# Group-norm means moved by one attention group, the start of the kernel reordered, and part of the last image's final convolution brought forward

## The chip, the cores and the metric

One core of one Trainium2 chip runs the kernel. The metric is device time in microseconds (us), lower is better.

The engines are named as in the profile: PE multiplies matrices, PEld loads its weights, DVE is VectorE, ACT is ScalarE, POOL is GpSimd, SP issues most DMAs.

## The reference

Eight images of 512 channels and 32 x 32 pixels pass through a group norm, a convolution block with two attention bottlenecks, and a residual addition. Everything is float32.

```python
def _L0_conv_ref(x, cv1_w, cv1_bn, cv2_w, cv2_bn, m_cv1_w, m_cv1_bn, m_qkv_w, m_rw, m_rh, m_cv2_w, m_cv2_bn):
    B, C1, C2, N, F, HEADS, E = (8, 512, 512, 2, 32, 4, 0.5)
    # C = 256, HD = 64; cbs = silu(batch norm(convolution))
    t = cbs(x, cv1_w, cv1_bn, 0)                       # 1x1, 512 -> 512
    ys = [t[:, :C], t[:, C:]]
    for i in range(N):
        yi = ys[-1]
        z = cbs(yi, m_cv1_w[i], m_cv1_bn[i], 1)        # 3x3, 256 -> 256
        z = bot_attention(z, m_qkv_w[i], m_rw[i], m_rh[i])   # 4 heads, 1024 positions
        z = silu(bn_eval(conv2d(z, m_cv2_w[i], 0), m_cv2_bn[i]))
        ys.append(yi + z)
    return cbs(concatenate(ys, axis=1), cv2_w, cv2_bn, 0)    # 1x1, 1024 -> 512

x = x + _L0_conv_ref(_gn(x), ...)      # _gn: 32 groups of 16 channels
```

## The kernel before

The kernel is a chain of stages, image by image: cv1 (1 x 1), a 3 x 3 convolution, attention, m2 (1 x 1), again a 3 x 3 convolution, attention and m2, then cv2. The 3 x 3 convolution is done in a transformed domain: `make_u` transforms the weights into "filters" (`u_new`), `tiles_in` transforms the image into "tiles" (`v_in`), PE multiplies the two, and `columns_out` and `rows_out` transform back. In image 0 the filters are made on DVE and ACT and stored; later images load them. An attention has four groups (pairs of heads by halves of the positions) of some 15 us each; between groups the function `ahead` slips in work for the next image, above all its group norm. `tc.issue_after(ins)` puts a block of instructions behind `ins` in the order in which the scheduler issues. A wait is always inferred from the data and is not written.

The group norm is a generator; each `yield` is a point where one attention group has passed:

```python
        def gn_mean(mv):
            ps = ps_big.tile([P, NX], F32, tag="big", name="gm_ps")
            nc.tensor.matmul(ps, gmat, mv[:, :, 0], start=True, stop=True)
            ...
        def group_norm(xts):
            ...
            stats(range(NX // 2))
            yield
            stats(range(NX // 2, NX))
            gm, dev = gn_mean(mv)          # PE needs the statistics just queued on DVE
            yield
            gr = gn_rstd(dev)
            apply(range(NX // 2), gm, gr)
            yield
            yield apply(range(NX // 2, NX), gm, gr)
```

The start. POOL issues sixteen small loads of BatchNorm parameters before it makes `gmat`, the matrix of the group means; the BatchNorm factors are computed before the group norm is emitted:

```python
    for i, src in enumerate(bn_chunks):          # 16 chunks
        nc.gpsimd.dma_start(bnp[:, i, :], src)
    ...
    ident = const.tile([P, P], F32, name="ident")
    make_identity(nc, ident)
    ...
    gmat = const.tile([P, P // GROUP, GROUP], F32, name="gmat")
    nc.gpsimd.memset(gmat, 1.0 / GROUP)
    ...
    nc.vector.tensor_scalar(rstd, bnp[:, :, 3], BN_EPS, None, ALU.add)
    nc.gpsimd.tensor_tensor(rstd, rstd, mhalf[:, :NBN], ALU.pow)
    nc.vector.tensor_tensor(sh, bnp[:, :, 0], rstd, ALU.mult)
    ...
    with tc.issue_after([*s.group_norm(xs)][-1].ins):
        make_all(0, 0)                           # filters of the first output half
    y0 = new_y0()
    s.cv1(w1, xs, y0, ypad[0], [*Y1S, *Y0S])
    vs = s.tiles_in(ypad[0])                     # free to mix with the filters
```

The last operation of `tiles_in` (output columns 0 and 3 of the transform in one instruction) and the products for V:

```python
                    tt(v[..., 0::3], pairs_of(0), pairs_of(2), ALU.subtract)
    ...
                for j in range(per):
                    for k in range(NM):
                        nc.tensor.matmul(
                            ps[:, j, :], z[:, k, ts(j0 + j, P)], qkv_sb[:, n, k, 2 * C : 3 * C],
                            start=(k == 0), stop=(k == NM - 1),
                        )
```

In an image that is not the last, pieces of the next image's cv1 (`first`, `second`, and two more behind m2) fill the end of the first attention. The last image has nothing to put there:

```python
        def first():
            nonlocal nxt
            if more:
                nxt = new_y0()
                s.cv1(w1, xs, nxt, y1n, Y1S[: NM // 2])
        def second():
            if more:
                s.cv1(w1, xs, nxt, y1n, Y1S[NM // 2 :])
        ...
        ao, check = s.attention_fast(0, z, ..., {**{g: ahead for g in range(NG)}, NG: first, NG + 1: second})
        last = s.m2(0, ao, y1, lambda oc, half: inner(y2, oc, half))
        if more:
            s.cv1(w1, xs, nxt, y1n, Y0S)
        vs = s.tiles_in(y2)
        ...
        z = s.conv3x3(1, vs, u_of(1))
```

## Time and profile before

| | before |
|---|---|
| time, median of 3 runs | 2547.76 us (2543.94 to 2548.48) |
| span of the profiled run, granted clock | 2543.0 us, 0.989 |
| PE busy, PE idle | 2436.7 us, 106.3 us |
| cv1 of image 0 begins | 25.04 us |
| first projections (end of the first 3 x 3 convolution) begin | 89.60 us |

PE is busy 96% of the span, so the question is where its 106 us of idleness lie and what each costs. The prediction shows those views. The group of the outer-column operation, by its form (count, busy time in us, mean ns of one), shows 1065 ns where the two inner columns, of half its size, take 421:

```profile
L330 DVE TENSOR_TENSOR v_in<-w_rows 128x512 f32<-128x512 f32 x96 | 102.3, 1065 | 0.0
```

The busy times of one stretch, from the first filter operation to the end of the first tiles (from:to, its length, then busy us and instructions of PE, PEld, DVE, ACT and POOL, the granted clock, the DMA share and GB/s), show DVE 30.16 of 33.31 us busy, 3.2 us idle, and the statistics row shows when the third of the four x tiles had come:

```profile
27.07:60.38 33.31, 33.31 (x106) 17.11 (x105) 30.16 (x69) 13.88 (x27) 2.40 (x11) 1.00 0.55 194
...
8.72 1.29 DVE L373 BATCH_NORM_STATS2 st<-x 128x6 f32<-128x512 f32 x2 [1.46 <-DMA x<-in_x_dram]
```

### The profile page before, as it was taken

The page shows a single profiled execution, that of the slowest core. Times are in us where ns is not written, and L with a number is a line of the kernel's source. Part 1 is how long each engine was busy: PE and PEld are TensorE (multiplying, and loading weights), DVE is VectorE, ACT ScalarE, POOL GpSimd, SP SyncE. Part 2 cuts the span into 40 slices and gives each one's busy share as a digit, 9 for nine tenths or more (in the row PEclk, how much of TensorE's full clock was granted, in tenths as well). Part 3 has the DMA queues.
Part 4 walks back from the last instruction along what each step waited for, and adds up shares of the span by engine and source line. Part 5 has one row for each costly group of instructions (what it writes and reads, how often), then busy time and mean ns, then how long its engine had stood idle before and what let it go on. Part 6 is the DMA issues. An engine that isn't in the chain of part 4 may idle for free.

```text
span 2543.0 us, 35923 instructions
## 1 busy us (share of the span) xinstructions
PE 2436.7 (96%) x14626; PEld 1213.0 (48%) x14626; DVE 1521.0 (60%) x2524; ACT 966.6 (38%) x1322; POOL 115.0 (5%) x379
## 2 busy tenths in 40 slices
PE   6889999999999999999999999999999999999898
PEld 3535446363463634536354363634536354363533
DVE  6678564765556664656556665566564665636662
ACT  2353522525234261343514434153432535326251
POOL 2000000000100001000010000100001000000001
PEclk9999999999999999999999999999999999999999
DMA  6223114040140402304032030502205021050101
GB/s 213 76 88 136 44 37 167 15 150 10 54 150 15 149 15 75 125 15 149 15 128 76 24 136 15 189 15 77 86 10 199 10 86 40 26 182 15 50 15 60
DMA packets 86188, 199.37 MB, mean 78 GB/s; under 512 B 32384, under 2 KB 42112, under 8 KB 73728
## 3 DMA queue, kind: packets, MB, share of 16 engines
q1 hardware_dynamic: 73696, 151.35, 17.4%
q0 software_dynamic: 12320, 45.66, 5.1%
q8 instruction: 117, 1.92, 0.3%
q14 instruction: 55, 0.45, 0.1%
HBM read 166.89 MB, written 30.08 MB: 77 GB/s over the span
## 4 chain that ended last, share of the span: by engine, by line
PE 81%; DVE 8%; ACT 4%; issue 2%; DMA 1%; SPq 0%; ACTq 0%; POOL 0%; DVEq 0%
PE ps L272 31%; PE av_ps L509 14%; PE l_ps L483 13%; PE c_ps L677 12%; PE m_ps L698 4%; PE v_ps L449 4%; ACT pt L487 3%; PE s_ps L526 2%; DVE acc L495 1%; DVE ao L517 1%; DVE st L373 1%; DMA rs<-r_dram 1%; ACT t L260 1%; ACT z L260 1%; DVE r_ends L364 0%
## 5 line engine op out<-in xcount | busy, mean ns | idle before, releaser
L487 ACT ACTIVATE pt<-l_ps 128x1024 f32<-128x1024 f32 x512 | 496.0, 1025 | 221.6 <-PE l_ps L483 221.6
L495 DVE TENSOR_TENSOR acc<-acc,pt 128x1024 f32<-128x1024 f32 x384 | 469.8, 1223 | 141.8 <-ACT pt L487 117.1
L509 PE MATMUL av_ps<-pt,vT 64*64 64x512 f32 x4096 | 491.4, 595 | 12.6 <-DVE ao L517 11.2
L483 PE MATMUL l_ps<-q,kr 64*64 64x512 f32 x4096 | 493.7, 597 | 4.3 <-ACT pt L487 4.3
L677 PE MATMUL c_ps<-v_in,u 128*128 128x128 f32 x2688 | 305.4, 276 | 10.3 <-issue 6.6
L677 PEld LDWEIGHTS c_ps<-v_in,u 128*128 128x128 f32 x2688 | 304.5, 193 | 18.0 <-issue 13.6
L509 PEld LDWEIGHTS av_ps<-pt,vT 64*64 64x64 f32 x4096 | 154.8, 134 | 312.1 <-issue 226.0
L483 PEld LDWEIGHTS l_ps<-q,kr 64*64 64x64 f32 x4096 | 155.1, 134 | 287.3 <-issue 266.4
L272 PE MATMUL ps<-z,qkv_sb 128*128 128x512 f32 x512 | 229.3, 595 | 7.3 <-ACT z L260 7.3
L272 PE MATMUL ps<-x,w 128*128 128x512 f32 x512 | 227.9, 602 | 2.2 <-DVE x L406 2.2
L272 PE MATMUL ps<-ypad,w 128*128 128x512 f32 x512 | 227.1, 594 | 0.0
L260 ACT ACTIVATE t<-ps,bh,sh 128x512 f32<-128x512 f32 x64 | 47.1, 775 | 310.6 <-PE ps L272 190.8
L493 DVE TENSOR_TENSOR acc<-pt 128x1024 f32<-128x1024 f32 x64 | 78.4, 1226 | 137.1 <-ACT pt L487 137.1
L272 PEld LDWEIGHTS ps<-x,w 128*128 128x128 f32 x512 | 97.1, 192 | 130.9 <-issue 125.2
L440 DVE TENSOR_TENSOR kr<-ps,rw_sb 128x512 f32<-128x512 f32 x64 | 41.2, 686 | 192.9 <-PE ps L272 192.9
L272 PEld LDWEIGHTS ps<-ypad,w 128*128 128x128 f32 x512 | 96.6, 190 | 125.1 <-issue 125.1
L743 DVE TENSOR_TENSOR t<-t,x_res 128x512 f32<-128x512 f32 x64 | 43.9, 692 | 181.9 <-ACT t L260 155.9
L272 PEld LDWEIGHTS ps<-z,qkv_sb 128*128 128x128 f32 x512 | 94.7, 190 | 114.1 <-issue 91.8
L533 ACT COPY s_row<-s_ps 128x512 f32<-128x512 f32 x128 | 68.7, 589 | 149.0 <-PE s_ps L526 149.0
L272 PE MATMUL ps<-y,w 128*128 128x512 f32 x256 | 118.0, 599 | 4.3 <-ACT t L260 4.3
L337 ACT COPY m<-c_ps 128x256 f32<-128x256 f32 x96 | 35.4, 369 | 223.2 <-PE c_ps L677 223.2
L272 PE MATMUL ps<-ylast,w 128*128 128x512 f32 x256 | 117.2, 595 | 0.0
(119 smaller groups left out, 2136.8 us busy)
## 6 DMA issues: line engine op xcount, KB each, us to landing
u<-u SPq DMA_DIRECT2D x84, 1024.0 KB
w<-in_cv_w_dram SPq DMA_DIRECT2D x24, 1024.0 KB
x<-in_x_dram SPq DMA_DIRECT2D x32, 512.0 KB
x_res<-in_x_dram POOLq DMA_DIRECT2D x64, 256.0 KB, 3.8
out_dram<-t POOLq DMA_DIRECT2D x62, 256.0 KB, 2.6
u<-u_new POOLq DMA_DIRECT2D x12, 1024.0 KB, 5.1
rs<-r_dram SPq DMA_DIRECT2D x96, 128.0 KB
raw<-in_m_cv_w_dram SPq DMA_DIRECT2D x8, 576.0 KB
```

Source lines behind the costliest of these rows:

```text
L260: return nc.scalar.activation(dst, src, AF.Silu, scale=sh[:, k : k + 1], bias=bh[:, k : k + 1])
L272: nc.tensor.matmul(ps[:, half, :], w_of(k), rhs_of(k, half), start=(k == 0), stop=(k == nk - 1))
L449: nc.tensor.matmul(ps[:, j, :], z[:, k, ts(j0 + j, P)], qkv_sb[:, n, k, 2 * C : 3 * C], start=(k == 0), stop=(k == NM - 1),)
L483: nc.tensor.matmul(ps[kh * HD : (kh + 1) * HD, hd, :], kr[r, c, o : o + HD], q[r, c, ts(half, HALF)], start=True, stop=True,)
L487: exp = nc.scalar.activation(pt[:, i], ps, AF.Exp, scale=SCALE)
L493: return nc.vector.tensor_tensor(accs[g], pt[:, 0], pt[:, 1], ALU.add)
L495: ins = nc.vector.tensor_tensor(accs[g], accs[g], pt[:, i], ALU.add)
L509: nc.tensor.matmul(avs[g][hd * HD : (hd + 1) * HD, kh, :], vT[r, j, o : o + HD], pt[r, i, hd, :], start=(j == 0), stop=(j == NJ - 1),)
L526: nc.tensor.matmul(ps[hd * HD : (hd + 1) * HD, kh, :], ones[r], acc[r, hd, :], start=True, stop=True,)
L533: nc.scalar.copy(row, ps[:, kh, :])
L677: nc.tensor.matmul(ps[:, row, col, :], us[i][:, k, row, col, :], vs[i][:, k, row, col, :], start=(k == 0), stop=(k == NM - 1),)
L698: nc.tensor.matmul(pss[oc][:, half, :], m2_sb[:, n, k, ts(oc, P)], ao[:, k, ts(half, HALF)], start=(k == 0), stop=(k == NM - 1),)
```

## The change

The intent is to take PE's idle stretches out. There are five parts: (1) the group mean is taken one group after its statistics, and all four tiles are normalised in the last group; (2) at the start `gmat` comes first on POOL, the BatchNorm loads become six and move to ACT, the factors are computed behind the group norm, the first raw filter is loaded ahead of cv1's weights, and the tiles are put behind the filters; (3) the outer-column operation goes column by column; (4) the V products alternate between two banks, so that two of them need only the first half of z; (5) in the last image, the first half of three of cv2's four output blocks (`cv2_part`) is computed in and behind the first attention, kept in SBUF and added at the end. The core of the diff, with cuts:

```diff
+    raws = [load_raw(0, 0, 0, "k")]
     w1 = load_w1()
...
-    for i, src in enumerate(bn_chunks):
-        nc.gpsimd.dma_start(bnp[:, i, :], src)
+        nc.scalar.dma_start(bnp[:, at:bn_at, :], src.rearrange("(c p) f -> p c f", p=P))
...
-                    tt(v[..., 0::3], pairs_of(0), pairs_of(2), ALU.subtract)
+                    outer = v_all[:, k, :, 0::3].rearrange("p r c (t j) -> p c r t j", j=NW)
+                    tt(outer, *(pairs_of(a).rearrange("p r t j b -> p b r t j") for a in (0, 2)), ALU.subtract)
...
             stats(range(NX // 2, NX))
+            yield
             gm, dev = gn_mean(mv)
             yield
-            gr = gn_rstd(dev)
-            apply(range(NX // 2), gm, gr)
-            yield
-            yield apply(range(NX // 2, NX), gm, gr)
+            yield apply(range(NX), gm, gn_rstd(dev))
...
-                for j in range(per):
+                in_bank = per // NH
+                for j in range(in_bank):
                     for k in range(NM):
+                        for at in range(j, per, in_bank):
...
-    with tc.issue_after([*s.group_norm(xs)][-1].ins):
-        make_all(0, 0)
+    normed = [*s.group_norm(xs)][-1]
+    with tc.issue_after(normed.ins):
+        nc.vector.tensor_scalar(rstd, bnp[:, :, 3], BN_EPS, None, ALU.add)
+        nc.gpsimd.tensor_tensor(rstd, rstd, mhalf[:, :NBN], ALU.pow)
+        nc.vector.tensor_tensor(sh, bnp[:, :, 0], rstd, ALU.mult)
+        ...
+        made = make_all(0, 0)
     y0 = new_y0()
     s.cv1(w1, xs, y0, ypad[0], [*Y1S, *Y0S])
-    vs = s.tiles_in(ypad[0])
+    with tc.issue_after(made.ins):
+        vs = s.tiles_in(ypad[0])
...
         def first():
...
+            else:
+                parts[1] = s.cv2_part(w1, (y0, y1), 1)
         def second():
...
+            else:
+                parts[2] = s.cv2_part(w1, (y0, y1), 2)
...
+        else:
+            for oc in range(3, NO):
+                parts[oc] = s.cv2_part(w1, (y0, y1), oc)
```

More of the change, by code (lines that the diff above doesn't have):

```diff
@@ L112, in load_w1, with load_w2 @@
         return w
-    def load_w2():
+    def load_w2(n=2):
         nk = (2 + N) * NM // 2
-        ws = [ring([P, nk, C2], f"w2_{i}") for i in range(2)]
+        ws = [ring([P, nk, C2], f"w2_{i}") for i in range(n)]
         for i, w in enumerate(ws):
@@ L119, in load_w2, with load_raw @@
         return ws
+    def load_raw(n, oc, k, tag, bufs=1):
+        raw = act.tile([P, 9, P], F32, tag=tag, name="raw", bufs=bufs)
+        nc.sync.dma_start(raw, m_cv1_w[n, ts(k, P), :, ts(oc, P)])
+        return raw
+    raws = [load_raw(0, 0, 0, "k")]
     w1 = load_w1()
-    bn_chunks = []
+    NBN = 2 * NM + 2 * N * NM + NO
+    bnp = const.tile([P, NBN, 4], F32, name="bnp")
+    bn_at = 0
     def bn_slot(src, n):
-        at = len(bn_chunks)
-        for c in range(n):
-            bn_chunks.append(src[ts(c, P), :])
+        nonlocal bn_at
+        at = bn_at
+        bn_at += n
+        nc.scalar.dma_start(bnp[:, at:bn_at, :], src.rearrange("(c p) f -> p c f", p=P))
         return at
-    bn_cv1 = bn_slot(cv1_bn, NX)
+    bn_cv1 = bn_slot(cv1_bn, 2 * NM)
     bn_m1 = [bn_slot(m_cv1_bn[n], NM) for n in range(N)]
@@ L134 @@
     bn_cv2 = bn_slot(cv2_bn, NO)
-    NBN = len(bn_chunks)
-    bnp = const.tile([P, NBN, 4], F32, name="bnp")
-    for i, src in enumerate(bn_chunks):
-        nc.gpsimd.dma_start(bnp[:, i, :], src)
     qkv_sb = const.tile([P, N, NM, 3 * C], F32, name="qkv_sb")
@@ L149, in load_bottleneck @@
         nc.sync.dma_start(m2_sb[:, n], m_cv2_w[n].rearrange("(k p) o -> p k o", p=P))
-    ident = const.tile([P, P], F32, name="ident")
-    make_identity(nc, ident)
-    ones = const.tile([P, HD], F32, name="ones")
-    nc.gpsimd.memset(ones, 1.0)
     gmat = const.tile([P, P // GROUP, GROUP], F32, name="gmat")
@@ L169 @@
     nc.gpsimd.memset(mhalf, -0.5)
+    ones = const.tile([P, HD], F32, name="ones")
+    nc.gpsimd.memset(ones, 1.0)
     ypad = []
@@ L175 @@
         yp = const.tile([P, NM, F + 2, F], F32, name=f"ypad{n}")
-        for c in range(NM):
-            nc.gpsimd.memset(yp[:, c, 0, :], 0.0)
-            nc.gpsimd.memset(yp[:, c, F + 1, :], 0.0)
+        nc.gpsimd.memset(yp[:, :, 0, :], 0.0)
+        nc.gpsimd.memset(yp[:, :, F + 1, :], 0.0)
         ypad.append(yp)
@@ L187 @@
     rstd = const.tile([P, NBN], F32, name="rstd")
-    nc.vector.tensor_scalar(rstd, bnp[:, :, 3], BN_EPS, None, ALU.add)
-    nc.gpsimd.tensor_tensor(rstd, rstd, mhalf[:, :NBN], ALU.pow)
-    nc.vector.tensor_tensor(sh, bnp[:, :, 0], rstd, ALU.mult)
-    nc.vector.tensor_tensor(bh, bnp[:, :, 2], sh, ALU.mult)
-    nc.vector.tensor_tensor(bh, bnp[:, :, 1], bh, ALU.subtract)
-    for at in bn_m1:
-        nc.vector.tensor_scalar(sh[:, at : at + NM], sh[:, at : at + NM], 1 / 48, None, ALU.mult)
     u_dram = [
@@ L204, in new_u, with make_u @@
         return ring([P, NM, 2, NC, P], name)
-    def make_u(n, oc, k, us, tag, raw_tag, bufs=(1, 1)):
-        raw = act.tile([P, 9, P], F32, tag=raw_tag, name="raw", bufs=bufs[1])
-        nc.sync.dma_start(raw, m_cv1_w[n, ts(k, P), :, ts(oc, P)])
+    def make_u(n, oc, k, us, tag, raw, bufs=1):
         g0, g1, g2 = (raw[:, 3 * r : 3 * r + 3, :] for r in range(3))
-        tmp = act.tile([P, 5, 3, P], F32, tag=tag, name="u_tmp", bufs=bufs[0])
+        tmp = act.tile([P, 5, 3, P], F32, tag=tag, name="u_tmp", bufs=bufs)
         both, other, rows = tmp[:, 0], tmp[:, 1], tmp[:, 2:4]
@@ L231, in make_u @@
             tt(u[:, :, 1, :], ends, c1, ALU.add)
-            tt(u[:, :, 2, :], ends, c1, ALU.subtract)
+            last = tt(u[:, :, 2, :], ends, c1, ALU.subtract)
             nc.scalar.mul(u[:, :, 0, :], c0, 2.0)
@@ L236, in make_u @@
                 nc.gpsimd.dma_start(u_dram[n][oc][i], us[i])
+        return last
     def load_u(n, oc, i):
@@ L264, in table_of, with conv1x1 @@
             nc.scalar.activation(spare, zero, func)
-        def conv1x1(w_of, rhs_of, nk, ks=None, ps=None):
+        def conv1x1(w_of, rhs_of, nk, ks=None, ps=None, ends=None):
             if ps is None:
                 ps = ps_big.tile([P, NH, HALF], F32, tag="big", name="ps")
+            begin, end = ends or (0, nk - 1)
             for k in range(nk) if ks is None else ks:
@@ L272, in conv1x1 @@
                     nc.tensor.matmul(
-                        ps[:, half, :], w_of(k), rhs_of(k, half), start=(k == 0), stop=(k == nk - 1)
+                        ps[:, half, :], w_of(k), rhs_of(k, half), start=(k == begin), stop=(k == end)
                     )
@@ L446, in project @@
                 ps = ps_big.tile([P, per, C], F32, tag="big", name="v_ps")
-                for j in range(per):
+                in_bank = per // NH
+                for j in range(in_bank):
                     for k in range(NM):
-                        nc.tensor.matmul(
-                            ps[:, j, :], z[:, k, ts(j0 + j, P)], qkv_sb[:, n, k, 2 * C : 3 * C],
-                            start=(k == 0), stop=(k == NM - 1),
-                        )
+                        for at in range(j, per, in_bank):
+                            nc.tensor.matmul(
+                                ps[:, at, :], z[:, k, ts(j0 + at, P)], qkv_sb[:, n, k, 2 * C : 3 * C],
+                                start=(k == 0), stop=(k == NM - 1),
+                            )
                 for g in range(0, per, per // NH):
@@ L707, in m2, with cv2_products @@
             return last
-        def cv2_products(w2, ys, oc, ks, ps=None):
+        def cv2_products(w2, ys, oc, ks, ps=None, ends=None):
             def cat(k, half):
@@ L716, in cv2_products, with cv2_part, cv2 @@
             nk = (2 + N) * NM
-            return conv1x1(lambda k: w2[2 * k // nk][:, k % (nk // 2), ts(oc, P)], cat, nk, ks, ps)
-        def cv2(b, w2, ys, begun=None):
+            return conv1x1(lambda k: w2[2 * k // nk][:, k % (nk // 2), ts(oc, P)], cat, nk, ks, ps, ends)
+        def cv2_part(w2, ys, oc):
+            ks = range(2 * NM)
+            ps = cv2_products(w2, ys, oc, ks, ends=(ks[0], ks[-1]))
+            part = act.tile([P, HW], F32, tag="x", name="part", bufs=NX)
+            for half in range(NH):
+                nc.scalar.copy(part[:, ts(half, HALF)], ps[:, half, :])
+            return part
+        def cv2(b, w2, ys, begun=None, parts={}):
             def rows_of(dram, oc, half):
@@ L736, in cv2 @@
                     ks = range((2 + N) * NM)
-                    if i == 0 and begun is not None:
+                    if oc in parts:
+                        ks = ks[2 * NM :]
+                        ps = cv2_products(w2, ys, oc, ks, ends=(ks[0], ks[-1]))
+                    elif i == 0 and begun is not None:
                         ps = cv2_products(w2, ys, oc, ks[-NM:], begun)
@@ L741, in cv2 @@
                 t = act.tile([P, HALF], F32, tag="t", name="t", bufs=2)
-                silu(t, ps[:, half, :], bn_cv2 + oc)
+                src = ps[:, half, :]
+                if oc in parts:
+                    nc.vector.tensor_tensor(t, src, parts[oc][:, ts(half, HALF)], ALU.add)
+                    src = t
+                silu(t, src, bn_cv2 + oc)
                 nc.vector.tensor_tensor(t, t, res.pop(0), ALU.add)
@@ L766, in make_all @@
         for k in range(NM):
-            make_u(n, oc, k, [us[oc, i] for i in range(PAIRS)], "q", "kv"[k])
-    with tc.issue_after([*s.group_norm(xs)][-1].ins):
-        make_all(0, 0)
+            raw = raws.pop(0) if raws else load_raw(n, oc, k, "kv"[k])
+            last = make_u(n, oc, k, [us[oc, i] for i in range(PAIRS)], "q", raw)
+        return last
+    normed = [*s.group_norm(xs)][-1]
[3 more added lines that the diff above has]
+        nc.vector.tensor_tensor(sh, bnp[:, :, 0], rstd, ALU.mult)
+        nc.vector.tensor_tensor(bh, bnp[:, :, 2], sh, ALU.mult)
+        nc.vector.tensor_tensor(bh, bnp[:, :, 1], bh, ALU.subtract)
+        for at in bn_m1:
+            nc.vector.tensor_scalar(sh[:, at : at + NM], sh[:, at : at + NM], 1 / 48, None, ALU.mult)
+        made = make_all(0, 0)
     y0 = new_y0()
     s.cv1(w1, xs, y0, ypad[0], [*Y1S, *Y0S])
-    vs = s.tiles_in(ypad[0])
+    with tc.issue_after(made.ins):
+        vs = s.tiles_in(ypad[0])
     load_bottleneck(0)
@@ L793 @@
             xs = [load_x(act, b + 1, c, NX) for c in range(NX)]
+        parts = {}
         norm = s.group_norm(xs) if more else iter(())
@@ L803, in ahead @@
             if g == 0:
-                if more:
-                    w1 = load_w1()
+                w1 = load_w1() if more else load_w2(1)
                 for at in ((0, 0), (0, 1), (0, 2), (1, 0)):
@@ L811, in ahead @@
             if b == 0 and g < NM:
-                make_u(1, 0, g, [us[0, i] for i in range(PAIRS)], "y0", "pt", (2, 3))
+                make_u(1, 0, g, [us[0, i] for i in range(PAIRS)], "y0", load_raw(1, 0, g, "pt", 3), 2)
         def first():
@@ L857 @@
                 vs = s.tiles_in(y1n)
-        s.cv2(b, w2, (y0, y1, y2, ylast), begun)
+        s.cv2(b, w2, (y0, y1, y2, ylast), begun, parts)
         y0 = nxt
@@ L882 @@
             g_big = gs.enter_context(tc.tile_pool(name="g_big", bufs=2, space=PSUM))
+            ident = g_act.tile([P, P], F32, name="ident")
+            make_identity(nc, ident)
             g_av = gs.enter_context(tc.tile_pool(name="g_av", bufs=2, space=PSUM))
```

## The prediction

> **What bounds it now.** I read the page first, then the waits of the matmul engine (PE), then its timeline, keeping only rows with a wait. From the page:
>
> ```profile
> PE 2436.7 (96%) x14626; PEld 1213.0 (48%) x14626; DVE 1521.0 (60%) x2524; ACT 966.6 (38%) x1322; POOL 115.0 (5%) x379
> PE 81%; DVE 8%; ACT 4%; issue 2%; DMA 1%; SPq 0%; ACTq 0%; POOL 0%; DVEq 0%
> ```
>
> PE works for 2436.7 of 2543.0 us and makes 81% of the chain that ended last. Every matmul of before is in after, so only PE's 106 us of idleness can go, with the slow matmuls that follow an idle stretch. PE's waits (who for whom, us in total, times, longest):
>
> ```profile
> PE gm_ps L379 <- DVE mv L374: 21.1, 7, 3.1
> PE gm_ps L379 <- POOL gmat L163: 14.6, 1, 14.6
> PE c_ps L677 <- ACT u_new L233: 9.3, 3, 6.5
> PE gv_ps L390 <- DVE dev L385: 7.0, 1, 7.0
> PE ps L272 <- ACT z L260: 7.3, 16, 0.5
> PE c_ps L677 <- issue: 6.6, 1, 6.6
> ```
>
> They fall into four kinds: the group-norm mean (gm_ps) once in each of the first seven images, the start (POOL's gmat, dev, the filters u_new), a half microsecond before the projections of each of 16 attentions, and one hole in the last image. The timeline shows the price of the first (start, duration, group, idle before):
>
> ```profile
> 461.75 0.56 PE L379 MATMUL gm_ps<-mv,gmat 128*128 128x4 f32 x2 [3.09 <-DVE mv L374]
> 462.24 3.69 PE L483 MATMUL l_ps<-q,kr 64*64 64x512 f32 x16
> ...
> 1080.12 0.36 PE L379 MATMUL gm_ps<-mv,gmat 128*128 128x4 f32 x2 [3.09 <-DVE mv L374]
> 1080.41 1.95 PE L483 MATMUL l_ps<-q,kr 64*64 64x512 f32 x16
> ```
>
> The same 16 matmuls last 3.69 us after one wait and 1.95 after another: sometimes the wait is paid twice. The start and the last image:
>
> ```profile
> 14.61 0.59 PE L379 MATMUL gm_ps<-mv,gmat 128*128 128x4 f32 x2 [14.61 <-POOL gmat L163]
> 18.06 0.17 DVE L188 TENSOR_SCALAR rstd<-bnp 128x16 f32<-128x16 f32 x1 [6.35 <-DMA bnp<-in_cv_bn_dram]
> 25.04 30.75 PE L272 MATMUL ps<-x,w 128*128 128x512 f32 x64 [2.22 <-DVE x L406]
> ...
> 2362.74 0.77 PE L677 MATMUL c_ps<-v_in,u 128*128 128x128 f32 x2 [6.60 <-issue]
> 2365.51 9.51 PE L677 MATMUL c_ps<-v_in,u 128*128 128x128 f32 x64 [2.00 <-DVE v_in L330]
> 2376.65 14.34 PE L677 MATMUL c_ps<-v_in,u 128*128 128x128 f32 x126 [1.62 <-DVE v_in L330]
> ```
>
> At 18.06 the BatchNorm factors, which nobody needs yet, wait for their data at the head of VectorE's (DVE's) queue, with the group mean behind them.
>
> **What the Trainium skill says.** "TensorE: Matmul & The Clock Gate", Part 1: after an idle window of about 3.4 us the array runs at half clock until it has been busy for about as long; the window runs freely. The trace agrees: after 3.09 us of idleness the double time shows in images 1, 2 and 6 of the range 1 to 6, not in 3 to 5. "Advanced Engine Details and Errata", SBUF Cachelines: a different 16-byte line at each access costs time. The outer-column operation alternates between two distant columns of its output; it takes 1065 ns for 512 elements, where other additions of 512 take 685, so the trace fits. "PSUM — Partial Sum Buffer", The four PSUM rules: two open accumulations in one bank spoil each other, which explains why the change pairs products of different banks; no run before shows it. "DMA: Bandwidth & Descriptors", Issuing engines are not separate DMA queues: moving the BatchNorm loads to another engine saves issue time only; POOL's 16 issues of 0.54 us are what delays gmat here.
>
> **Part by part.**
>
> *Group means a group later.* Statistics of the second half stay in attention group 1; the mean goes to group 2; the normalisation of all four tiles goes to group 3. A group lasts some 15 us and the statistics end 3 us late, so images 1 to 6 lose 6 x 3.09 = 18.5 us of waiting. The slow stretch after it I measure from the mean to the next wait for ao: 15.84, 14.41, 12.76, 12.76, 12.76, 15.72 us, hence 3.1 + 1.65 + 3.0 = 7.7 us of excess. Clock windows are a matter of luck, and VectorE now does four 0.8 us normalisations in a row in group 3, so I count 6. Sum 24.5. In image 0 VectorE is also making filters in groups 0 and 1: eight additions of 1.23 us less one, statistics 2.5 and filters 5.9 are some 17 us against 15 of PE. There the 2.58 us wait mostly turns into another wait for VectorE: 2.
>
> *Start.* Gmat is first on POOL and the BatchNorm arithmetic is behind the normalisation. The statistics ended at 11.71 us; then matmul, copy, three small operations, matmul, power (1.03) and one normalisation take about 4.3 us by their own durations: cv1 starts at 16, not 25, 9 us earlier. From there VectorE, not PE, sets the end of the first convolution: it was busy nearly without a pause from 24 to 72, and PE waited 6.46 and 1.69 us for u_new, then ran slowly (90 products in 12.9 us, against 192 in 21.6 later). VectorE starts 9 us earlier, pays the factors behind it (about 1.5, more if it waits for the power of 2.9), and saves 6 x 0.37 on outer columns: 9.0 - 1.5 + 2.2 = 9.7. Making filters before tiles, with the first raw filter loaded early, should take out a little of its pauses: 11.5 in all. The early raw filter delays cv1's weights by 0.59 MB, or 1.6 us at the 360 GB/s seen; with 3.7 MB ahead of it they land near 13.5, before 16.
>
> *Outer columns.* 96 operations go from 1065 to about 687 ns: 36 us of VectorE, nearly all beside PE. It counts where PE waits for VectorE: above, in image 0's second convolution (waits 0.82 + 3.01 + 1.13 and 2.5 us of slowness; 2.2 us less work: 3), and in the last image.
>
> *V products.* PE can now run two first-half products before it needs the second half of z: 0.43 us more work in a hole of 0.46, 16 times: 6.9. Copies of the first bank start later; I see no one waiting.
>
> *Last image.* Three quarters of the first half of cv2, 3 x 8 matmuls of 0.86 us or 3 x 6.87 us, move into the first attention. No PE work vanishes. From 2346.60 to the end of the convolution at 2390.8 PE took 44.2 us; its work there at full clock is 0.86 + 6.87 + 21.44 = 29.2: 15 us lost. The third part (6.87) covers the 6.60 us hole; of the tile waits 1.5 + 1.1 should remain, since each outer-column operation saves 0.37 and the savings add up along the chain (the second tile 0.74 earlier, the fourth 1.5): 12 gained. ScalarE's six copies and VectorE's six additions lie beside PE, except one 0.69 us addition in the last tail: -0.7.
>
> Sum: 24.5 + 2 + 11.5 + 3 + 6.9 + 12 - 0.7 = 59.2; 2547.76 - 59.2 = 2488.6, rounded to **2488**.
>
> **Rivals.** (1) *The wait moves.* Group 3 gets 3.2 us of normalisation between additions, and the exponentials' buffers come free late. For: only three pairs of buffers, and image 0 shows such stalls. Against: group 1 carried 2.5 us of statistics in before with only 0.24 us of waiting behind. If it cost 3 us in seven images: 2509. (2) *VectorE remains the bound of the start and eats the 9 us*: the matmul starts early but filters and tiles in series end no sooner, because the power stalls DVE and small loads slow x. For: VectorE's near-full row from 24 to 72. Against: all its work is released earlier. The time would be about 2497. (3) *More than counted*: filters first, so that the second half's are ready when PE gets there; then the first convolution saves 17 to 19 us and the time is about 2481. (4) *The filler is useless*, because its copies delay the last image's silu, or it lies behind a buffer wait: 2500.
>
> **Range and chances.** Firm are the waits of images 1 to 6 (18.5), the projections (7) and the last image's hole (about 7 of 12): 32 us. The rest, 27, hangs on the scheduler's order and on clock luck, good for half as much either way; the runs before spread by 4.5 us. So 2470 to 2506. Two per cent is 51 us, at about 2497, 9 us from my middle: faster 0.75, same 0.24, slower 0.01.
>
> **What would show it.** Right: no gm_ps row among PE's waits beyond the start; gmat ready before 12 us and cv1 at 16; outer columns near 690 ns; z waits below 0.1 us; no 6.6 us hole before the last image's second convolution. Wrong: new waits of l_ps or av_ps for pt or ao in group 3; first projections still near 89 us; waits of PE for part copies; or a granted clock below the 0.989 of before.

## The result, and the profile after

| | before | after |
|---|---|---|
| time, median of 4 runs each | 2546.74 us (2543.94 to 2548.48) | 2502.78 us (2498.81 to 2504.16) |
| ratio, 95% interval | 1 | 0.9826 (0.9809 to 0.9843) |
| profiled span, granted clock | 2543.0 us, 0.989 | 2497.3 us, 0.994 |
| PE busy, idle | 2436.7, 106.3 us | 2424.1, 73.2 us |

A ratio is the mean time of one kernel's runs over that of the other's of the same rounds, so it is not quite the ratio of the medians quoted. All outputs are right. The change made the kernel 44 us, or 1.7%, faster; it stayed short of 2%. Of the 45.7 us between the two profiles, 33.1 are less idleness of PE and 12.6 are less busy time for the same 14626 matmuls; the granted clock rose with it, from 0.989 to 0.994, so fewer of them ran slowly.

The page of after shows PE nearer to its limit: DVE's share of the last chain fell from 8% to 5%, POOL's small share has gone.

```profile
PE 2424.1 (97%) x14626; PEld 1208.3 (48%) x14626; DVE 1497.6 (60%) x2530; ACT 969.9 (39%) x1328; POOL 104.6 (4%) x355
PE 86%; DVE 5%; ACT 3%; issue 2%; DMA 1%; SPq 0%; ACTq 0%; DVEq 0%
```

PE's waits of after (who for whom, us in total, times, longest). The mean waits for the statistics once, at the start, and no more in the images. The half microsecond before the projections, 7.3 us in total, is no longer among the rows. What grew is `u_new`, from 9.3 to 12.7 us, and `ao`, from 11.2 to 14.4:

```profile
PE av_ps L505 <- DVE ao L513: 14.4, 32, 3.6
PE gm_ps L374 <- DVE mv L369: 13.0, 1, 13.0
PE c_ps L673 <- ACT u_new L224: 12.7, 4, 8.3
PE l_ps L479 <- ACT pt L483: 7.3, 3, 4.3
PE c_ps L673 <- DVE v_in L325: 5.0, 4, 1.6
PE c_ps L673 <- DVE r_ends L336: 2.3, 1, 2.3
```

PE's timeline of after at the mean in image 1, which is now one group later. Before had 3.09 us of waiting there and then 3.69 us for 16 matmuls; after has no wait, and 1.95 us.

```profile
466.37 0.39 PE L374 MATMUL gm_ps<-mv,gmat 128*128 128x4 f32 x2
466.68 1.95 PE L479 MATMUL l_ps<-q,kr 64*64 64x512 f32 x16
```

Two groups of after, by their form: the outer columns take 691 ns each, and the projections' idle time ahead of them is 0.4 us in all.

```profile
L325 DVE TENSOR_TENSOR v_in<-w_rows 128x512 f32<-128x512 f32 x96 | 66.3, 691 | 0.0
L266 PE MATMUL ps<-z,qkv_sb 128*128 128x512 f32 x512 | 229.3, 595 | 0.4
```

The start of after on PE's timeline. cv1 begins at 17.22 (25.04 before), but then PE waits 1.09, 8.26, 0.93 and 2.24 us:

```profile
17.22 30.25 PE L266 MATMUL ps<-x,w 128*128 128x512 f32 x64 [2.22 <-DVE x L401]
...
55.92 3.87 PE L673 MATMUL c_ps<-v_in,u_new 128*128 128x128 f32 x32 [1.09 <-DVE v_in L325]
68.04 0.80 PE L673 MATMUL c_ps<-v_in,u_new 128*128 128x128 f32 x2 [8.26 <-ACT u_new L224]
...
72.80 12.27 PE L673 MATMUL c_ps<-v_in,u_new 128*128 128x128 f32 x90 [2.24 <-ACT u_new L224]
```

The last image of after. The hole of 6.60 us is filled, and three waits for tiles stand in front of the convolution's products:

```profile
2341.49 3.84 PE L673 MATMUL c_ps<-v_in,u 128*128 128x128 f32 x32 [1.65 <-DVE v_in L325]
2346.58 3.84 PE L673 MATMUL c_ps<-v_in,u 128*128 128x128 f32 x32 [1.25 <-DVE v_in L325]
2351.47 14.34 PE L673 MATMUL c_ps<-v_in,u 128*128 128x128 f32 x126 [1.06 <-DVE v_in L325]
```

To say where the time came from, I cut PE's timeline of both kernels at the same instructions and took the difference of each stretch:

| step of the prediction | predicted, us | between the two profiles, us |
|---|---|---|
| group means, first attentions of images 1 to 6 | 24.5 | 25.3 (6.19, 3.95, 2.96, 3.13, 2.99, 6.08) |
| image 0's first attention | 2 | 0.1 |
| start, up to the first projections | 11.5 | 4.7 |
| image 0's second 3 x 3 convolution | 3 | 1.0 |
| V products, 16 projections | 6.9 | 6.9 |
| last image, first attention's end to the second projections | 12 | 9.6 |
| tail | -0.7 | -0.5 |
| second attentions (longer waits for ao in some) | 0 | -1.4 |
| sum | 59.2 | 45.7 |

Two steps, the group means and the V products, carry 32.2 of the 45.7 us and are as predicted. The start is the large miss: 6.8 of the 13.5 us that are lacking.

### The profile page after: what moved, and what is told of

It reads as the page before. It is cut to its first block, busy times and chain, and to the rows that moved or that the text cites. A ratio compares the mean times of both kernels' runs of the same rounds, so it can differ in the third digit from the quotient of the medians.

```text
span 2497.3 us, 35914 instructions
## 1 busy us (share of the span) xinstructions
PE 2424.1 (97%) x14626; PEld 1208.3 (48%) x14626; DVE 1497.6 (60%) x2530; ACT 969.9 (39%) x1328; POOL 104.6 (4%) x355
## 4 chain that ended last, share of the span: by engine, by line
PE 86%; DVE 5%; ACT 3%; issue 2%; DMA 1%; SPq 0%; ACTq 0%; DVEq 0%
PE ps L266 34%; PE av_ps L505 15%; PE l_ps L479 14%; PE c_ps L673 13%; PE v_ps L445 4%; PE m_ps L694 4%; ACT pt L483 2%; PE s_ps L522 2%; DVE ao L513 1%; DVE acc L489 1%; DMA rs<-r_dram 1%; ACT t L252 1%; DVE acc L491 1%; DMA r_dram<-rc 0%; DVE v_in L325 0%
## 5 line engine op out<-in xcount | busy, mean ns | idle before, releaser
L505 PE MATMUL av_ps<-pt,vT 64*64 64x512 f32 x4096 | 485.4, 591 | 16.6 <-DVE ao L513 14.4
L479 PE MATMUL l_ps<-q,kr 64*64 64x512 f32 x4096 | 485.7, 592 | 7.3 <-ACT pt L483 7.3
L673 PEld LDWEIGHTS c_ps<-v_in,u 128*128 128x128 f32 x2688 | 302.6, 192 | 11.2 <-issue 6.7
```

The costliest lines, as they stand in the source:

```text
L479: nc.tensor.matmul(ps[kh * HD : (kh + 1) * HD, hd, :], kr[r, c, o : o + HD], q[r, c, ts(half, HALF)], start=True, stop=True,)
L505: nc.tensor.matmul(avs[g][hd * HD : (hd + 1) * HD, kh, :], vT[r, j, o : o + HD], pt[r, i, hd, :], start=(j == 0), stop=(j == NJ - 1),)
L673: nc.tensor.matmul(ps[:, row, col, :], us[i][:, k, row, col, :], vs[i][:, k, row, col, :], start=(k == 0), stop=(k == NM - 1),)
```

## Theories and experiments

*The start.* Theory: DVE's queue, not PE, sets the end of image 0's first convolution, and the change puts three obstacles into it: the BatchNorm factors stop the queue for POOL's power; the tiles may no longer fill the pauses of the filters; and the x tiles come later, because POOL, with the sixteen issues and the power no longer in front of them, sends the two residual loads (`x_res`) at once. The views of after that suggest it are the same stretch as above, from the first filter operation to the end of the first tiles, the waits of DVE in 19 to 40.1 us, and the early timeline:

```profile
19.33:55.86 36.53, 35.50 (x128) 19.46 (x127) 29.16 (x75) 14.46 (x29) 5.52 (x12) 1.00 0.60 213
```

```profile
DVE sh L788 <- POOL rstd L787: 2.8, 1, 2.8
DVE u_tmp L221 <- ACT u_tmp L217: 2.1, 2, 1.1
DVE u_tmp L208 <- ACT u_new L225: 1.5, 1, 1.5
```

```profile
2.72 1.22 POOL L735 DMA_DIRECT2D x_res<-in_x_dram  x2
9.93 1.29 DVE L368 BATCH_NORM_STATS2 st<-x 128x6 f32<-128x512 f32 x2 [2.10 <-DMA x<-in_x_dram]
```

DVE begins its filters 7.74 us earlier than before (19.33 for 27.07) and has 1.0 us less work in the stretch (29.16 for 30.16), yet it ends only 4.5 us earlier (55.86 for 60.38), since its idle time in the stretch grew from 3.2 to 7.4 us. The rival theory: PE's slow clock or the weights of cv1 hold the start, and DVE's order matters little.

*Image 0's attention.* In the first two groups DVE also makes the filters of the second convolution. Theory A: these bursts on DVE delay its additions and so the return of the exponentials' buffers; they cost about the same wherever PE happens to wait. Theory B: the raw filters themselves take one of the three buffers that the exponentials (`pt`) use.

*The last image.* Theory: the filler of `second` stands in front of m2, so everything behind m2, tiles included, starts too late; behind m2 the same products would cover the tiles. Rival: there is a new wait for ao if m2 has nothing in front of it.

The kernels, each with its own control in the same job (the medians of before in the three jobs were 2547.95, 2544.89 and 2547.98 us):

| kernel | time, median (range), us | ratio to before (95%) |
|---|---|---|
| after, run again | 2501.95 (2500.01 to 2503.94) | 0.9823 (0.9808 to 0.9838) |
| before with the means alone | 2522.71 (2518.78 to 2524.71) | 0.9901 (0.9886 to 0.9916) |
| after without the outer columns | 2507.95 (2507.54 to 2509.1) | 0.9855 (0.9837 to 0.9872) |
| tiles free | 2500.03 (2495.44 to 2500.81) | 0.9814 (0.98 to 0.9828) |
| factors early | 2498.53 (2495.71 to 2500.3) | 0.9813 (0.9794 to 0.9832) |
| residual loads late | 2501.47 (2499.46 to 2501.93) | 0.9826 (0.9808 to 0.9844) |
| start: all four edits | 2497.12 (2492.08 to 2498.91) | 0.9804 (0.9787 to 0.9822) |
| filters in groups 0 and 2 | 2498.95 (2494.67 to 2500.21) | 0.9809 (0.9795 to 0.9823) |
| raw filters in their own buffers | 2501.78 (2500.64 to 2502.71) | 0.983 (0.9812 to 0.9848) |
| filler late | 2497.02 (2492.88 to 2500.54) | 0.9802 (0.9788 to 0.9816) |
| start edits and filler late | 2490.2 (2489.3 to 2494.27) | 0.9782 (0.9766 to 0.9798) |
| the same, filters cut in six | 2485.73 (2483.49 to 2486.59) | 0.9758 (0.9743 to 0.9773) |

### After, run again

No edit; it shows what two profiles of one kernel differ by.

> The changed kernel itself once more, as the yardstick of this set: 0.981 to 0.984 of the kernel before. My theory of image 0's attention (one wait of 3.6 us at the end of group 1, after which PE is slow or not by luck) expects that this profile may well show the slow stretch behind that wait (av_ps of 16 products in 3.3 to 3.7 us instead of 1.95) that the first profile of this kernel lacked; the attention of image 0 then takes 78 us and not 75.

Measured: 2501.95 us. The span of this profile is 2502.5 us, against 2497.3 of the first, for the same kernel. The first projections begin at 85.24 instead of 84.90, and image 0's attention takes 77.87 instead of 75.10 us. The difference begins in one row; in the first profile of after it was the same wait, 3.56 us, and then 1.95 us:

```profile
154.19 3.69 PE L505 MATMUL av_ps<-pt,vT 64*64 64x512 f32 x16 [3.59 <-DVE ao L513]
```

The matmuls behind a wait of 3.6 us run slowly in one profile and fast in the other. So a single profile of these kernels is uncertain by up to 3 us for each such wait, and the 0.1 us gained in image 0's attention was luck: the usual value is a loss of 2.7 us. The first projections vary too: the five profiles here whose start is that of after have them at 84.72 to 85.76 us.

### The group means alone

```diff
 before
             stats(range(NX // 2, NX))
-            gm, dev = gn_mean(mv)
             yield
-            gr = gn_rstd(dev)
-            apply(range(NX // 2), gm, gr)
+            gm, dev = gn_mean(mv)
             yield
-            yield apply(range(NX // 2, NX), gm, gr)
+            yield apply(range(NX), gm, gn_rstd(dev))
```

> The kernel before with the group means a group later and nothing else. My theory (the waits for the mean, 18.5 us in images 1 to 6, vanish, and with them the slow matmuls after them, 6 to 8 us by luck; image 0 gains next to nothing because VectorE bounds it): 23 to 27 us faster than before, no row of gm_ps among PE's waits after the start, and the first attention of images 1 to 6 at 59.5 us from the first logits to the end of av instead of 62.7 to 65.8. Rival (the wait moves into group 3, where four normalisations stand in a row): less than 12 us, and new waits for pt or ao in the last group.

Measured: 2522.71 us, 25 us faster than before. The first attentions of images 1 to 6 take 59.54 to 60.54 us, where before they took 62.67 to 65.74. In image 0 it takes 77.9 us instead of 75.2. So this part alone gives 25 of the change's 44 us, and its loss of 2.7 us in image 0 is its own, not an effect of the other parts.

### The outer columns undone

```diff
 after
-                    outer = v_all[:, k, :, 0::3].rearrange("p r c (t j) -> p c r t j", j=NW)
-                    tt(outer, *(pairs_of(a).rearrange("p r t j b -> p b r t j") for a in (0, 2)), ALU.subtract)
+                    tt(v[..., 0::3], pairs_of(0), pairs_of(2), ALU.subtract)
```

> The changed kernel with the outer columns in their old order of dimensions: 96 operations back from 0.69 to 1.06 us. Theory (36 us of VectorE, nearly all beside PE): slower by 4 to 8 us only: 2 to 3 in the first convolution, about 2 in image 0's second convolution, about 1.5 in the last image's waits for tiles; nothing in images 1 to 6. Rival (VectorE's time in the middle images matters after all): slower by more than 12 us.

Measured: 2507.95 us; by the ratios (0.9855 for 0.9826) some 7 us slower than after. The first projections begin at 87.51 (84.90 in after), and image 0's second convolution has its waits of before again, on PE's timeline:

```profile
237.90 0.77 PE L672 MATMUL c_ps<-v_in,u_new 128*128 128x128 f32 x2 [3.01 <-DVE r_ends L335]
```

The operation saves 36 us of DVE and about 7 us of time. Against the first profile of after 2.6 us of that lie in the start, 1.3 in image 0's second convolution and 1.7 in the last image's tiles: it counts only where PE waits for DVE.

### The start: tiles free of the filters

```diff
 after
-    with tc.issue_after(made.ins):
-        vs = s.tiles_in(ypad[0])
+    vs = s.tiles_in(ypad[0])
```

> The changed kernel without the constraint that puts the first input tiles behind the first filters on VectorE. Theory (the constraint left VectorE idle for some 6 us between 19 and 40 us, in its waits for ScalarE and GpSimd, which tile work filled before): the first projections start 3 to 5 us earlier than at 84.9 us. Rival (the interleaving delays the filters, and the constraint is what won the 4.7 us): they start 1 us or more later than at 84.9.

Measured: 2500.03 us. The first projections begin at 81.59, 3.3 us earlier than in after. The longest wait is 4.59 instead of 8.26 us:

```profile
65.56 0.80 PE L673 MATMUL c_ps<-v_in,u_new 128*128 128x128 f32 x2 [4.59 <-ACT u_new L224]
```

DVE's waits for ACT before `u_tmp` L221, 4.6 us in four places of after, are 2.1 us in two. In all DVE stands idle for 9.4 instead of 12.0 us between its first filter operation and the first projections. This is one of the change's own edits undone, and undoing it is a gain at the place it was made for. In the total it gives about 3 us as well (0.9814 for 0.9826), although the intervals of the two ratios overlap.

### The start: factors early

```diff
 after
-    normed = [*s.group_norm(xs)][-1]
-    with tc.issue_after(normed.ins):
-        nc.vector.tensor_scalar(rstd, bnp[:, :, 3], BN_EPS, None, ALU.add)
-        nc.gpsimd.tensor_tensor(rstd, rstd, mhalf[:, :NBN], ALU.pow)
+    norm0 = s.group_norm(xs)
+    next(norm0)                      # the first two statistics
+    nc.vector.tensor_scalar(rstd, bnp[:, :, 3], BN_EPS, None, ALU.add)
+    nc.gpsimd.tensor_tensor(rstd, rstd, mhalf[:, :NBN], ALU.pow)
+    normed = [*norm0][-1]
+    with tc.issue_after(normed.ins):
```

> The changed kernel with the sum and the power of the BatchNorm factors put after the statistics of the first two tiles of x, so that GpSimd's power of 3.15 us runs while x still lands. Theory (behind the normalisation that power stops VectorE for 2.80 us at the head of the chain of filters and tiles that ends the first convolution): the 2.80 us idle is gone and the first projections start 2 to 3.5 us earlier than at 84.9 us, provided the loads of the BatchNorm data have landed by about 8 us. Rival (VectorE has slack there, because filters wait for ScalarE and PE anyway): less than 1 us. If the data land late, cv1 starts later than at 17.2.

Measured: 2498.53 us; DVE's wait of 2.80 us for the power is gone, because POOL computes it while DVE waits for x. The first projections begin at 81.83, 3.1 us earlier, and the ratio is lower by as much (0.9813 for 0.9826). The parameters had landed at 7.56 us, so the factors need not stand behind the group norm. But the edit does a second thing, which its expectation overlooked: the residual loads now stand behind the power in POOL's queue and are issued at 10.90 instead of 2.72 us.

```profile
10.90 1.26 POOL L735 DMA_DIRECT2D x_res<-in_x_dram  x2
```

The statistics end at 11.96 instead of 12.85 us and the filters begin 0.9 us earlier, so up to 0.9 of the 3.1 us may come from the earlier x and not from the power. A new limit appears on PE's timeline: cv1 now waits for its weights.

```profile
16.73 29.26 PE L266 MATMUL ps<-x,w 128*128 128x512 f32 x64 [2.63 <-DMA w<-in_cv_w_dram]
```

### The start: residual loads late

```diff
 after
-        nc.gpsimd.tensor_tensor(rstd, rstd, mhalf[:, :NBN], ALU.pow)
+        powed = nc.gpsimd.tensor_tensor(rstd, rstd, mhalf[:, :NBN], ALU.pow)
...
-        s.cv2(b, w2, (y0, y1, y2, ylast), begun, parts)
+        with tc.issue_after(powed.ins) if b == 0 else ExitStack():
+            s.cv2(b, w2, (y0, y1, y2, ylast), begun, parts)
```

> The changed kernel with the first two residual loads (0.5 MB, needed only 200 us later) held behind the power of the BatchNorm factors. Theory (GpSimd, freed from its 16 issues, now starts them at 2.7 us, where they take bandwidth from x, so the statistics end at 12.85 us and not at 11.7): the statistics end near 11.7 and cv1 starts near 16.1 instead of 17.2; the first projections 1 us earlier. Rival (x is slower because of the small BatchNorm loads on ScalarE's queue): no change of cv1's start.

Measured: 2501.47 us. POOL issues the residual loads at 21.13 instead of 2.72, the third x tile is there at 8.47 instead of 9.93, and the statistics end at 11.39 instead of 12.85. cv1 begins only 0.9 us earlier, since it is then the weights that it waits for, and the first projections 0.7 us earlier, which is less than the spread of 84.72 to 85.76 in kernels with one start. The effect of the loads on x is shown, since nothing else was edited; its effect on the projections and on the total is too small to see.

```profile
8.47 1.29 DVE L368 BATCH_NORM_STATS2 st<-x 128x6 f32<-128x512 f32 x2 [0.52 <-DMA x<-in_x_dram]
...
16.30 30.78 PE L266 MATMUL ps<-x,w 128*128 128x512 f32 x64 [2.77 <-DMA w<-in_cv_w_dram]
```

### The start: all four

The three edits above and cv1's weights ahead of the raw filter (the two lines that the change had put the other way round):

```diff
-    raws = [load_raw(0, 0, 0, "k")]
     w1 = load_w1()
+    raws = [load_raw(0, 0, 0, "k")]
```

> The changed kernel with four things at the start: cv1's weights loaded before the first raw filter, residual loads held back, sum and power of the BatchNorm factors among the statistics, and tiles free to mix with filters. Theory (each term found alone: 2.8 us power, 3.3 us order, 1.5 us of x and weights): cv1 starts at 15 to 15.8 us, the first projections at 76.5 to 79.5 instead of 84.9, so that the start gains 10 to 13 us over before, the 11.5 of the prediction; the whole time is 5 to 8 us under the changed kernel. Rival (the terms fill the same idle time of VectorE and do not add up): projections at 80.5 or later.

Measured: 2497.12 us; the first projections begin at 79.81 (80.90 and 80.76 in the two later kernels with the same start). cv1 begins at 16.33, so both expectations, 15 to 15.8 and 76.5 to 79.5, were missed by a little. The wait for weights is gone, and the three gains of 3.3, 3.1 and 0.7 us do not add up: some 5 us of 7.6 (half a microsecond of it reckoned for the weights) arrive. In part they were counted twice: the residual loads go at 10.90 us, exactly as with the factors early alone, so the third edit adds nothing to the second. Another part is visible on DVE: its wait for ACT at 27.32 us is 2.96 us long, where factors early and tiles free each had 1.07 for that wait, since ACT now has cv1's first silu in front of that filter operation. What is left on PE's timeline is DVE making the second half's filters:

```profile
64.55 0.80 PE L673 MATMUL c_ps<-v_in,u_new 128*128 128x128 f32 x2 [5.15 <-DVE u_tmp L221]
```

So the rival theory has a small part of the truth: once the statistics end earlier, the weights hold cv1, by some 0.5 us, but DVE's order is what most of the time hangs on. PE's slow stretch at the end, 90 products in 12.27 us in after and 12.93 in before, costs about the same in both. Against before the start now gains 8.7 to 9.8 us. The prediction of 11.5 was near what the parts can give with their order mended, and it was not what the change gave.

### Image 0: filters in groups 0 and 2

```diff
 after
-            if b == 0 and g < NM:
-                make_u(1, 0, g, [us[0, i] for i in range(PAIRS)], "y0", load_raw(1, 0, g, "pt", 3), 2)
+            if b == 0 and g % 2 == 0:
+                make_u(1, 0, g // 2, [us[0, i] for i in range(PAIRS)], "y0", load_raw(1, 0, g // 2, "pt", 3), 2)
```

> The changed kernel, but image 0 makes its two half filters for the second bottleneck in attention groups 0 and 2 instead of 0 and 1. Theory (in image 0 VectorE is over its budget of 15 us in groups 0 and 1: 17 and 18 us of work; so the vanished wait for the mean came back as waits for pt and ao): the 75.1 us of that attention fall by 3 to 8 us, the waits of PE for ao at the end of group 1 (3.56 us) and for pt in it (1.73, 0.79, 1.35) vanish, and the whole time falls by 3 to 8 us. Rival (the waits come from the buffers that the raw filter borrows from the exponentials, wherever it stands): the same number of waits, one group later, and a change under 2 us.

Measured: 2498.95 us, and 75.13 us for image 0's attention. The waits of 1.39 and 4.26 us in group 0 stay. The three for pt in group 1 go, and 0.79 us for ao is left of 3.56, but others appear in group 2 (2.26 us for the mean's copy, 1.98 for ao), where the mean's copy now stands behind the filters in DVE's queue, and slow matmuls follow:

```profile
154.03 1.36 PE L479 MATMUL l_ps<-q,kr 64*64 64x512 f32 x8 [2.26 <-DVE gm L377]
155.15 3.38 PE L505 MATMUL av_ps<-pt,vT 64*64 64x512 f32 x16
```

The waits follow the filters from group to group, which theory A expects. PE's waits in that attention sum to 10.7 us instead of 13.3, but slow matmuls eat what that gave against the first profile of after; against the usual 77.9 us it is a gain of 2.7 us. The predicted fall of 3 to 8 us did not come, so the run alone is inconclusive on how much there is to gain.

### Image 0: raw filters in their own buffers

```diff
 after
+    def load_raw_ring(n, oc, k):
+        raw = ring([P, 9, P], "raw")             # the ring of the weights, not the exponentials' buffers
+        nc.sync.dma_start(raw, m_cv1_w[n, ts(k, P), :, ts(oc, P)])
+        return raw
...
-                make_u(1, 0, g, [us[0, i] for i in range(PAIRS)], "y0", load_raw(1, 0, g, "pt", 3), 2)
+                make_u(1, 0, g, [us[0, i] for i in range(PAIRS)], "y0", load_raw_ring(1, 0, g), 2)
```

> The changed kernel with the two raw filters of image 0's first attention in a free buffer of the weights' ring instead of one of the three buffers of the exponentials. Theory A (the filters' bursts of VectorE work stop the additions, and the borrowed buffer does little): the waits for pt in groups 0 and 1 (1.39, 4.26, 1.73, 0.79, 1.35 us) shrink by less than a third; total within 2 us. Theory B (the borrowed buffer leaves two for the exponentials, so every burst of VectorE reaches PE): the waits shrink by more than half and the attention of image 0 takes 68 to 71 us instead of 75.1; 4 to 7 us gained.

Measured: 2501.78 us and 78.0 us for image 0's attention, as in the second profile of after. The longest wait for an exponential is the same to the hundredth, and theory B falls:

```profile
124.93 1.98 PE L484 MATMUL l_ps<-q,kr 64*64 64x512 f32 x8 [4.26 <-ACT pt L488]
```

That theory B falls does not show theory A's route, from late additions to late buffers. ACT's timeline of after shows another: ACT makes a part of the filters (`u_new`) too, and here such an operation stands in its queue, waiting for DVE, with an exponential behind it:

```profile
117.03 0.42 ACT L224 ACTIVATE u_new<-u_tmp 128x256 f32<-128x256 f32 x1 [3.76 <-DVE u_tmp L210]
117.35 0.40 ACT L225 ACTIVATE u_new<-u_tmp 128x256 f32<-128x256 f32 x1
117.66 1.00 ACT L483 ACTIVATE pt<-l_ps 128x1024 f32<-128x1024 f32 x1
```

The logits of that exponential were complete at 113.03 us, and it goes into a buffer that its pair has used since 112.24, so neither logits nor a buffer held it. The exponential that ends the wait of 4.26 us stands behind two such operations, which waited 2.04 and 1.60 us for DVE. It runs at 123.86 in after and at 123.87 here, where it has a third buffer. So DVE's filter work reaches PE through ACT's queue at least in these two places; no run moves ACT's part of the filters, so what that would give is not known.

### The last image: filler late

```diff
 after
         def second():
...
-            else:
-                parts[2] = s.cv2_part(w1, (y0, y1), 2)
...
-            for oc in range(3, NO):
+            for oc in range(2, NO):
                 parts[oc] = s.cv2_part(w1, (y0, y1), oc)
```

> The changed kernel with the second of the three filler parts of the last image moved from before the second matmul of attention to behind it. Theory (one part of 6.87 us is too short to cover the tiles, hence the 1.65 + 1.25 + 1.06 us of waits; nothing before the second matmul needs the filler for more than 0.75 us): the three waits vanish, a wait of about 0.8 for ao comes back, 3 us gained in the last image. Rival (VectorE's tiles are late whatever PE does, since the copies of the filler on ScalarE delay silu): the waits stay, no gain.

Measured: 2497.02 us. From the last image's first logits to the next projections it takes 109.36 instead of 113.72 us, 4.4 us less. The three waits for tiles are gone, no wait for ao took their place, and all 192 products of the convolution stand in one row of PE's timeline:

```profile
2345.24 21.60 PE L673 MATMUL c_ps<-v_in,u 128*128 128x128 f32 x192
```

### The start edits and the late filler together

The edit is the sum of the two before it.

> start_best and the filler part moved behind the second matmul (4 us alone). Theory (the two are in different images and add up): 9 to 13 us under the changed kernel, some 2489 to 2493 us, 2.1 to 2.4% under before. Rival (clock luck in image 0 eats the start's gain, as it did where tiles were free): 3 to 6 us under the changed kernel.

Measured: 2490.2 us, 2.2% faster than before and 12 us faster than after in the same rounds. The gains of the start (5 in its own run) and of the filler (4.4 in its stretch) add up to a little less than that, so no loss of the one to the other is seen.

### The same, with image 0's filters cut in six

The filters of the second convolution have two input halves of three pieces each. They are made one, two, one and two pieces in the four groups, instead of three and three in the first two:

```diff
             nc.scalar.mul(u[:, :, 3, :], c2, 2.0)
             if k == NM - 1:
                 nc.gpsimd.dma_start(u_dram[n][oc][i], us[i])
-        return last
+            yield last
...
-            if b == 0 and g < NM:
-                make_u(1, 0, g, [us[0, i] for i in range(PAIRS)], "y0", load_raw(1, 0, g, "pt", 3), 2)
+            if b == 0:
+                if g % 2 == 0:
+                    steps.append(make_u_steps(1, 0, g // 2, [us[0, i] for i in range(PAIRS)], "y0", load_raw_ring(1, 0, g // 2), 2))
+                for _ in range(1 + g % 2):
+                    next(steps[-1])
```

> best, with the two half filters of image 0's first attention cut into six pieces spread over four groups (1, 2, 1, 2), their raw data in the weights' ring. Theory (bursts of 8 us of VectorE work between two additions stop PE there, and the long wait makes PE slow after it): image 0's attention from 78 to 66 to 71 us, 5 to 10 us under best. Rival (the work does not fit whatever its grain): under 2 us.

Measured: 2485.73 us, 2.4% faster than before and 16 us faster than after. Image 0's attention takes 72.51 us instead of 77.89 in the kernel without this edit. The waits became shorter and more even (1.31, 1.53, 3.14, 1.96, 1.18, 1.80 and 1.18 us), and none of them has slow matmuls behind it. But their sum hardly fell, from 13.3 to 12.1 us: of the 5.4 us gained in this attention 4.2 are less busy time of PE, that is fewer slow matmuls, so smaller bursts mostly saved the second price of the waits and not the waits. The 4.5 us in the total and the 72.5 us are both short of what was expected (5 to 10, and 66 to 71). The longest wait that remains, and what ACT does before the exponential that ends it:

```profile
136.07 1.09 PE L487 MATMUL l_ps<-q,kr 64*64 64x512 f32 x8 [3.14 <-ACT pt L491]
...
134.58 0.52 ACT L212 ACTIVATE u_tmp<-raw 128x384 f32<-128x384 f32 x1 [3.04 <-DMA raw<-in_m_cv_w_dram]
```

Here ACT stood for 3.04 us with a filter operation at the head of its queue whose raw filter SP had only requested at 130.04 us. An earlier load is the next thing to try; no run did.

It is the best kernel.

## Why the prediction was right or wrong

The time, 2502.78 us, lies in the predicted range of 2470 to 2506. It lies 15 us above the middle (the sum of 2488.6 rounds to 2489, not 2488), and the likeliest outcome, faster by over 2%, did not come: the gain was 1.7%.

- **What bounds the kernel** was right: PE's idle stretches and the slow matmuls behind them. Of the 45.7 us gained between the profiles 12.6 are busy time of PE, so reckoning the wait alone would have missed over a quarter.
- **Group means in images 1 to 6** were right in mechanism and size: 24.5 predicted, 25.3 between the profiles, 25 for the part alone. Rival 1, that the wait moves into group 3, did not happen there: with the means alone those attentions became uniform, at 59.5 to 60.5 us.
- **Image 0's attention** was mis-sized: "There the 2.58 us wait mostly turns into another wait for VectorE: 2." More than all of it turned into other waits: their sum in this attention rose from 11.4 to 13.3 us, and the last of them, about 3.6 us for ao, has slow matmuls behind it in most profiles. The step measured 0.1 with luck and -2.7 without.
- **V products** were right to the tenth: 6.9 us.
- **Start.** This is the step that failed, 4.7 us for 11.5 (3.8 to 4.9 over the five profiles with this start). The first half of it nearly held: cv1 began 7.8 us earlier, not 9, because the statistics ended at 12.85 instead of 11.71. The step "a little of its pauses", for filters before tiles, had the wrong sign: the order took away the work that filled DVE's pauses behind ACT, and restoring it gave 3.3 us. The factors, "about 1.5, more if it waits for the power of 2.9", did wait for it, and the edit that took that wait out gave 3.1 us, up to 0.9 of it by letting x in earlier. The weights of cv1 land at about 16.3 to 16.7, not near 13.5, as the two runs with earlier statistics show. Rival 2, "VectorE remains the bound of the start and eats the 9 us", named two of the causes in advance, the power and slower x, and put the time at about 2497; that it was slowed by the residual loads and not by the small BatchNorm loads I had not seen.
- **Image 0's second convolution** gave 1.0 for 3. Its waits shrank only from 0.82 + 3.01 + 1.13 to 2.33 + 1.28 us: the 0.37 us saved in each outer-column operation shortens a chain in which other DVE work stands too; no run took that chain apart.
- **Outer columns**: "from 1065 to about 687 ns", measured 691; undoing them costs about 7 us.
- **Last image** gave 9.6 for 12. The filler did cover the hole, but its second piece also pushed the tiles back, so three waits remained, 3.96 us in all, where 1.5 + 1.1 were reckoned. Rival 4, the useless filler, is refuted by these 9.6 us.
- **Clock.** "Clock windows are a matter of luck" was right, and it also limits the proof here: the two profiles of after differ by 5.2 us.

Three things stay open. The three start edits together fall short of their sum by 2 to 2.5 us; about 0.7 of it is the effect of the residual loads counted twice, and the rest is not divided among them. The -1.4 us in the second attentions is in both profiles of after, but in the later kernels it ranges from none to 1.9, so its cause is not known. Image 0's attention, at its best 72.5 us, is still 13 us above the 59.5 of the others; 12.1 of these are the seven waits listed above, and how much of them would go if ACT's part of the filters were moved or loaded earlier was not tried.

## What to carry to other kernels

When PE is 96% busy, list its idle stretches, ask of each who is late, and give that engine's work one more group of slack; where the wait is 3 us or longer, count the slow matmuls behind it as well (here they followed 3 of 6 waits of 3.09 us and most longer ones). Before forcing an order on the engine that bounds a stretch, look whether what you push back was filling its pauses, and keep an instruction that waits for another engine (here a 3 us power, and filter operations in front of exponentials) out of the head of its queue. Moving issues off an engine lets its later issues out earlier, so look what those will compete with.

## What the Trainium skill lacked or had wrong

- "TensorE: Matmul & The Clock Gate", Part 1, gives an idle window of about 3.4 us after which the clock falls, with a free-running phase. In the runs here a wait of 3.09 us was already followed by the double time in three of six images, and waits of 3.55 to 4.29 us, always in the same place of image 0's attention, were followed by slow matmuls in 9 of 11 profiles (3.69 us for 16 of them in eight, 3.28 in one, 1.95 in two); a wait of 4.26 us in the same attention had them behind it in all 13 profiles that have it. What the page lacks is the chance of it for a wait near 3.4 us.
- "Advanced Engine Details and Errata", SBUF Cachelines, says that a different line at each access costs time and gives no figure. Here one DVE instruction of 512 elements per partition took 1065 ns with its output alternating between two distant columns and 691 ns column by column, although its inputs then went from neighbouring elements to every second one.
- "DMA: Bandwidth & Descriptors", Issuing engines are not separate DMA queues, says that issuing from several engines saves only the time to issue. That is so for each transfer, but moving the sixteen issues, and the power behind them, out of the way on POOL let its next ones start at 2.72 instead of 21.47 us, and these delayed the third x tile from 8.72 to 9.93 us (8.47 when they were held back).
- No page gives the time of a power on GpSimd: it took 2.93 to 3.15 us for 128 x 16 elements and 1.03 to 1.04 us for 128 x 4.
